# Row sums added to a row of the column products by two transfers, in place of a spread on a diagonal

## The chip, the cores and the metric

The kernel runs on one core of a Trainium2 chip. Its engines work side by side, each through its own list of instructions in order: TensorE (PE, matmuls), VectorE (DVE), ScalarE (ACT), GpSimd (POOL) and SyncE (SP, which here only issues transfers). The metric is the device time of one execution in microseconds (us); less is better.

## The reference

Input `x` is 4 images of 64 channels of 256x256 numbers. Layer 0 convolves each channel with its own long 2-D filter `k`, an outer product of two decaying curves that small networks make from `z` (`hx`, `hy`), and adds a bias:

```python
k = einsum('ijk,imk->ijmk', hx, hy)            # one separable filter per channel
out = irfft2(rfft2(x) * rfft2(k) / fft_size) + x * bias[:, None, None]
```

Layer 1 weighs the products of the rows of each image with each other, sums them, adds the sum to each row, and normalises the channel:

```python
scores = einsum('bpsd,bptd->bpst', x, x) / sqrt(256)
red = sum(scores * weights[None], axis=-1, keepdims=True)
y = x + red
y_hat = (y - mean) * rsqrt(var + 1e-5)         # mean, var over images, rows, columns
return y_hat * gamma + beta
```

## The kernel before

The 64 channels are handled one after another in a loop (lines 662 to 709); the last two run through `last_channels` with an order of their own. Within a channel the filter's separability makes the convolution two rounds of matmuls with triangular Toeplitz blocks (`toep`): `conv_z` (line 211) into `z`, copied out of PSUM by ACT (line 220), and `conv_x0` (line 236), to which DVE adds the bias (line 246), giving `x0`.

`gram` (line 299) multiplies the rows of `x0` with each other, in two halves `v`, two images in each, into PSUM. The scores are symmetric, so only some blocks of 64x64 are computed. `weigh` then uses each block twice: once summed along its rows (line 328, two instructions per image, whose accumulated sums go to two columns of `red0`), and once as products that are still to be summed down the columns (line 319, into `pr`, 256 numbers per partition and image).

The two kinds of sum are put together as follows. `spread` (line 340, four instructions of 128x128 after each half) multiplies the identity by the two row sums, so that each partition's row sum lies on the diagonal, and adds `pr`, into `sp`. `all_sum` (line 348) is one all-reduce over the partitions on GpSimd, of 1024 numbers each: it gives all partitions the full sums, `rd`. In the next iteration of the loop ACT copies half of `rd` in place (`pick_red`, line 357), and DVE adds `rd` to `x0` with two passes of 128x1024 (`add_red`, line 364), which also accumulate the channel's sum. A small all-reduce (line 368) follows, then on ACT the mean (lines 411 and 412) and the squares (line 416), on GpSimd `sum_squares` (line 422), and later the root, the newton steps and the output (`finish`, line 462).

The order on every engine is written out by hand (`tc.manual_schedule()`): an engine takes its instructions as the program lists them and waits at the first that isn't ready. For DVE and channel c that is: adding the bias (four instructions), newton steps of channel c-3, weighing and spreading of c's first half, `add_red` of c-1, weighing and spreading of c's second half. For POOL: `sum_squares` of c-2, the small reduction of c-1, `all_sum` of c. For ACT, `pick_red` of c-1 stands behind the copies of `z` and ahead of the root of c-2.

All matmul results share a pool `ps` of eight PSUM banks, given out in turn, two each for the two halves of `conv_x0`, of `conv_z` and of `gram`. `sp`, `pr` and `rd` have two buffers each. SP issues all loads and stores of the loop. The channels from 61 on (`BY_PE`) use matmuls for the sums instead, except that the first half of 61 still goes through `spread` and `all_sum`.

Of the kernel before, what the change touches and what calls it, by code (L numbers as in the profile page):

```python
# [8 lines left out]
F32 = mybir.dt.float32  # L9
AF = mybir.ActivationFunctionType  # L10
ALU = mybir.AluOpType
# [4 lines left out]
B, C, S = 4, 64, 256  # L16
P = 128
# [20 lines left out]
def conv_scores_bn_kernel(  # L38
# [19 lines left out]
    nc = tc.nc  # L58

    const = ctx.enter_context(tc.tile_pool(name="const", bufs=1))  # L60
    dram = ctx.enter_context(tc.tile_pool(name="dram", bufs=1, space=DRAM))
    ld = ctx.enter_context(tc.tile_pool(name="ld", bufs=3))
    wk = ctx.enter_context(tc.tile_pool(name="wk", bufs=2))
    sm = ctx.enter_context(tc.tile_pool(name="sm", bufs=3))
# [3 lines left out]
    def load_xt(c, v, n):  # L68
        if not n:
            xts[c, v] = ld.tile([P, 4, S], F32, tag=f"xt{v}", name=f"xt_{c}_{v}", bufs=4)  # L70
        part = bass.ts(n, 2)
        nc.sync.dma_start(xts[c, v][:, part], xT[c, v, :, part])
# [45 lines left out]


    g_dram = dram.tile([COPIES, C, 2, GW], F32, name="g_dram")  # L120

    hs[0] = ld.tile([P, 2, GW], F32, tag="toep", name="toep_0")
    with tc.tile_pool(name="fps", bufs=4, space=PSUM) as fps:
# [54 lines left out]
    def load_h(c, n):  # L178


        if not n:
            hs[c] = ld.tile([P, 2, GW], F32, tag="toep", name=f"toep_{c}")
        src = bass.AP(
            g_dram.tensor, g_dram.offset + c * 2 * GW + 16 * n,
            [[4 + C * 2 * GW, COPIES], [1, 4], [1, GW + S]],
        )
        rows = hs[c][bass.ts(n, 16)].rearrange("p a r -> p (a r)")
        nc.sync.dma_start(rows[:, : GW + S], src)

    def copy_h(c):  # L190

        toep = hs[c]
        nc.scalar.copy(toep[H:, :, :S], toep[:H, :, :S])  # L193
# [5 lines left out]
    st8, zs = {}, {}  # L199
# [22 lines left out]
    def conv_x0(c, z, parts=range(2)):  # L222


        toep = hs[c]
        if not c:
            first_x0(z)
            return
        for m in parts:
            p2 = [ps.tile([P, 2, S], F32, tag="ps", name=f"p2_{c}_{m}_{v}") for v in range(2)]  # L230
            for i in range(2):
                for k in range(4):
                    for t in range(4):
                        v, u = t % 2, t // 2
                        rows = bass.ts(v, H)
                        nc.tensor.matmul(  # L236
                            p2[v][bass.ts(u, H), i, : S - H * k],
                            lhsT=z[rows, u, k, bass.ts(2 * m + i, H)],
                            rhs=toep[rows, 0, H * k : S], start=(k == 0), stop=(k == 3),
                        )  # L240
            add_bias(c, m, p2)
# [31 lines left out]

    def begin(c):
        x0 = wk.tile([P, 2, 4, S], F32, tag="x0", name=f"x0_{c}", bufs=5)
        red0 = sm.tile([P, B, 2], F32, tag="red0", name=f"red0_{c}")
        sp = wk.tile([P, B, S], F32, tag="sp", name=f"sp_{c}")
        pr = wk.tile([P, B, S], F32, tag="pr", name=f"pr_{c}")
        rd = wk.tile([P, B, S], F32, tag="rd", name=f"rd_{c}")
        st8[c] = (x0, red0, sp, pr, rd)  # L280
# [3 lines left out]
    def gram(c, v, weighed=True):  # L284


        xb = st8[c][0].rearrange("p v i (t s) -> p v i t s", s=H)
        gs = [ps.tile([P, 8, H], F32, tag="ps", name=f"g_{c}_{v}_{u}") for u in range(2)]

        for places in (  # L290
            ((0, slice(0, 3), slice(0, 5, 2)), (1, slice(1, 4), slice(2, 7, 2))),
            ((2, slice(2, 4), slice(3, 7, 3)), (3, slice(0, 4, 3), slice(0, 4, 3))),
        ):
            for i in range(4):
                for n in range(4):
                    u, h = n % 2, n // 2
                    rows = bass.ts(u, H)
                    m, t, o = places[h]
                    nc.tensor.matmul(  # L299
                        gs[u][bass.ts(h, H), o, :],  # L300
                        lhsT=xb[rows, v, i, m, :], rhs=xb[rows, v, i, t, :],
                        start=(i == 0), stop=(i == 3),
                    )
        if not weighed:
            banks.extend(gs)
            return
        for u in range(2):
            weigh(c, 2 * v + u, gs[u])
        if c < BY_PE or (c == BY_PE and not v):
            for u in range(2):  # L310
                spread(c, 2 * v + u)

    def weigh(c, b, g, rows_last=True):

        _, red0, _, pr, _ = st8[c]
        w = ws[c]

        def products():
            nc.vector.scalar_tensor_tensor(  # L319
                pr[:, b].rearrange("p (t s) -> p t s", s=H), g[:, COL, :], 1.0 / math.sqrt(S),  # L320
                w[:, 6:10, :], ALU.mult, ALU.mult,
            )

        if not rows_last:
            products()
        for n, part in enumerate((ROW0, ROW1)):
            junk = wk.tile([P, 3, H], F32, tag="junk", name=f"junk_{c}_{b}_{n}")
            nc.vector.scalar_tensor_tensor(  # L328
                junk, g[:, part, :], 1.0 / math.sqrt(S), w[:, 3 * n : 3 * n + 3, :],
                ALU.mult, ALU.mult, accum_out=red0[:, b, n : n + 1],  # L330
            )
        if rows_last:
            products()

    def spread(c, b):

        _, red0, sp, pr, _ = st8[c]
        for n in range(2):
            part = bass.ts(n, P)
            nc.vector.scalar_tensor_tensor(  # L340
                sp[:, b, part], eye_sb, red0[:, b, n : n + 1], pr[:, b, part],
                ALU.mult, ALU.add,
            )

    def all_sum(c, part=slice(0, B)):

        _, _, sp, _, rd = st8[c]
        nc.gpsimd.partition_all_reduce(  # L348
            rd[:, part].rearrange("p b s -> p (b s)"), sp[:, part].rearrange("p b s -> p (b s)"),
            P, RED.add,  # L350
        )
# [20 lines left out]
    BY_PE = C - 3  # L372
# [37 lines left out]
    def minus_mean(mom):  # L410
        nc.scalar.activation(mom[:, 4:5], mom[:, 2:3], AF.Identity, bias=mom[:, 3:4])  # L411
        nc.scalar.activation(mom[:, 5:6], mom[:, 4:5], AF.Identity, scale=-1.0 / (B * S * S))

    def squares(c, mom, v):
        sq = wk.tile([P, 4, S], F32, tag="sq", name=f"sq_{c}_{v}", bufs=1)
        nc.scalar.activation(  # L416
            sq, st8[c][0][:, v], AF.Square, bias=mom[:, 5:6], accum_out=mom[:, 6 + v : 7 + v]
        )
# [24 lines left out]
    def scale_shift(c, mom, v, r):  # L443
        return scale_shift_of(c, mom, newton(c, v, r))
# [204 lines left out]
    def parts_of(c, place):  # L649

        e, f = c - 4, c - 3
        parts = [[(e, 0, 1)], [(e, 1, 0)], [(e, 1, 1)], [(f, 0, 0)], []]
        if c >= C - 4:
            parts[4] = [(f, 0, 1)]
        if c == C - 3:
            parts[0] = []
            parts[4] += [(f, 1, 0), (f, 1, 1)]
        for i, v, n in parts[place]:
            if i >= 0:
                finish(*fins[i], v, n)  # L660

    for c in range(C - 2):
        p, q, f = c - 1, c - 2, c - 3
        begin(c)
        copy_h(c + 1)
        parts_of(c, 0)
        if c + 2 < C and c:
            load_xt(c + 2, 1, 1)
        load_h(c + 2, 0)
        conv_x0(c, zs.pop(c))  # L670
        if q >= 0:
            minus_mean(moms[q])
            squares(q, moms[q], 0)
        parts_of(c, 1)
        if c + 3 < C:
            load_xt(c + 3, 0, 0)
        load_h(c + 2, 1)
        if q >= 0:
            squares(q, moms[q], 1)
            tot = sum_squares(q, moms[q])  # L680
        if f >= 0:
            fins[f] = (f, *scale_shift(f, moms.pop(f), *scales.pop(f)))
        begin_z(c + 1)
        copy_z(c + 1, 0, conv_z(c + 1, 0))
        parts_of(c, 2)
        load_h(c + 2, 2)
        if c + 3 < C:
            load_xt(c + 3, 1, 0)
        load_w(c + 1)
        load_h(c + 2, 3)  # L690
        copy_z(c + 1, 1, conv_z(c + 1, 1))
        if p >= 0:
            pick_red(p)
        parts_of(c, 3)
        if c + 3 < C:
            load_xt(c + 3, 0, 1)
        if q >= 0:
            scales[q] = root(q, tot)
        if c == C - 3:
            copy_h(c + 2)  # L700
        parts_of(c, 4)
        gram(c, 0)
        if p >= 0:
            moms[p] = add_red(p)
        if c == BY_PE:
            all_sum(c, slice(0, 2))
        gram(c, 1)
        if c < BY_PE:
            all_sum(c)
    last_channels(C - 1)  # L710

# [70 lines left out]
```

## Time and profile before

Three runs took 883.51, 889.34 and 885.22 us (median 885.22). The profiled execution:

| | us | share of the span |
|---|---|---|
| span, first to last instruction | 872.5 | |
| PE busy | 855.9 | 98% |
| DVE busy | 755.9 | 87% |
| ACT busy | 621.9 | 71% |
| POOL busy | 427.8 | 49% |
| `all_sum`, 62 times | 376.8, 6.08 each | |
| `spread`, 492 instructions | 139.0, 0.34 each | |

The page gives the profiled execution's span; the median of the runs lies 12.7 us above it, for what stands around the first and last instruction. A busy time counts an instruction from its start to its end, and neighbours on one engine overlap a little: four spreadings of 0.34 take 1.13 together. In the timeline a line has start, duration, engine, line, operation and `out<-in`; in square brackets stand the idle time of the engine before it and what ended it. An engine name with a q (SPq, ACTq) is the queue's issuing of a transfer, not its landing.

### The profile page before, as it was taken

What the parts mean: (1) busy time and instruction counts of PE and PEld (TensorE: products, weight loads), DVE (VectorE), ACT (ScalarE), POOL (GpSimd) and SP (SyncE); (2) the same over time, 40 slices, a digit from 0 to 9 for tenths busy, and PEclk for the clock granted to TensorE, in tenths of its full rate; (3) what the DMA queues carried; (4) which work ended last, traced back from release to release, by engine and by line L of the source; (5) the groups of instructions that cost most, each with busy time, mean ns of one, the idle gap of its engine ahead of it and who ended that gap; (6) DMA issues with size and microseconds to landing.
All of it is one profiled execution on the core that took longest, in us unless ns stands there. A gap on an engine that the chain in (4) does not pass through costs nothing.

```text
span 872.5 us, 55963 instructions
## 1 busy us (share of the span) xinstructions
PE 855.9 (98%) x24674; PEld 836.2 (96%) x24674; DVE 755.9 (87%) x2647; ACT 621.9 (71%) x1218; POOL 427.8 (49%) x194
## 2 busy tenths in 40 slices
PE   7999999999999999999999999999999999999995
PEld 5999999999999999999999999999999999999994
DVE  3588988988988988988998998998998988988996
ACT  2256767767767767777777777777777767767786
POOL 0236546546546546546546546546546546546530
PEclk9999999999999999999999999999999999999997
DMA  6724665565565556565565565655555655565535
GB/s 189 221 77 139 198 209 195 201 211 193 201 210 192 200 196 206 202 207 193 203 208 192 203 206 194 205 200 199 203 201 199 202 203 192 204 210 193 190 141 194
DMA packets 89870, 169.69 MB, mean 194 GB/s; under 512 B 10555, under 2 KB 11740, under 8 KB 89628
## 3 DMA queue, kind: packets, MB, share of 16 engines
q1 hardware_dynamic: 88972, 165.52, 55.6%
q8 instruction: 194, 3.18, 1.6%
q10 hardware_dynamic: 656, 0.59, 0.3%
q14 instruction: 48, 0.39, 0.2%
HBM read 98.18 MB, written 67.76 MB: 190 GB/s over the span
## 4 chain that ended last, share of the span: by engine, by line
PE 97%; DVE 2%; DMA 1%; issue 0%; ACT 0%; DVEq 0%; ACTq 0%
PE p L211 32%; PE g L299 32%; PE p L236 32%; PE p L265 0%; DMA toep<-g_sb 0%; PE ph L132 0%; DVE junk L328 0%; DMA zw_sb<-in_zw 0%; PE rp L379 0%; DVE fa L135 0%; DVE x L516 0%; DVE pr L319 0%; PE rp L384 0%; PE s L507 0%; DVE fa L140 0%
## 5 line engine op out<-in xcount | busy, mean ns | idle before, releaser
L348 POOL PARTITION_ALL_REDUCE rd<-sp x62 | 376.8, 6078 | 182.4 <-DVE sp L340 182.4
L211 PE MATMUL p<-toep,xt 64*64 64x256 f32 (+3 forms) x8192 | 304.0, 296 | 0.9 <-DMA toep<-g_sb 0.9
L299 PE MATMUL g<-x 64*64 64x192 f32 (+1 forms) x8192 | 302.5, 296 | 0.0
L211 PEld LDWEIGHTS p<-toep,xt 64*64 64x64 f32 x8192 | 291.4, 133 | 8.6 <-PE idle L168 1.5
L236 PE MATMUL p<-toep,z 64*64 64x256 f32 (+3 forms) x8064 | 298.3, 296 | 0.0
L236 PEld LDWEIGHTS p<-toep,z 64*64 64x64 f32 x8064 | 289.6, 133 | 6.8 <-issue 0.2
L299 PEld LDWEIGHTS g<-x 64*64 64x64 f32 x8192 | 289.7, 133 | 0.8 <-DVE x L246 0.2
L328 DVE SCALAR_TENSOR_TENSOR junk<-g,w 128x192 f32<-128x192 f32 x512 | 160.9, 351 | 81.1 <-PE g L299 77.7
L462 ACT ACTIVATE o<-x,sh,g 128x512 f32<-128x512 f32 x252 | 203.3, 810 | 3.0
L246 DVE SCALAR_TENSOR_TENSOR x<-xt,chan_sb,p 128x512 f32<-128x512 f32 x256 | 173.8, 739 | 7.6 <-PE p L265 7.2
L220 ACT COPY z<-p 128x512 f32<-128x512 f32 x256 | 134.7, 576 | 22.3 <-PE p L211 22.3
L416 ACT ACTIVATE sq<-x,mom 128x1024 f32<-128x1024 f32 x127 | 145.2, 1143 | 3.3 <-DVE x L405 1.1
L364 DVE SCALAR_TENSOR_TENSOR x<-x,rd 128x1024 f32<-128x1024 f32 x122 | 144.1, 1218 | 0.0
L340 DVE SCALAR_TENSOR_TENSOR sp<-eye_sb,red,pr 128x128 f32<-128x128 f32 x492 | 139.0, 344 | 0.0
L368 POOL PARTITION_ALL_REDUCE mom<-mom x61 | 24.5, 401 | 231.1 <-DVE x L364 227.1
L357 ACT COPY rd<-rd 64x512 f32<-64x512 f32 (+1 forms) x62 | 38.0, 612 | 134.8 <-POOL rd L348 134.7
L319 DVE SCALAR_TENSOR_TENSOR pr<-g,w 128x256 f32<-128x256 f32 x256 | 107.3, 419 | 0.0
L193 ACT COPY toep<-toep 64x512 f32<-64x512 f32 x63 | 38.9, 617 | 32.0 <-DMA toep<-g_dram 26.7
L411 ACT ACTIVATE mom<-mom 128x1 f32<-128x1 f32 x62 | 18.2, 293 | 38.0 <-POOL mom L368 37.1
L328 DVE DVE_READ_ACCUMULATOR junk<-g,w 128x1 f32 x512 | 42.2, 82 | 0.0
L422 POOL PARTITION_ALL_REDUCE tot<-mom x62 | 29.8, 481 | 5.1 <-ACT sq L416 5.1
L416 ACT ACTIVATION_READ_ACCUMULATOR sq<-x,mom 128x1 f32 x127 | 23.7, 186 | 0.0
(84 smaller groups left out, 220.4 us busy)
## 6 DMA issues: line engine op xcount, KB each, us to landing
xt<-in_xT SPq DMA_DIRECT2D x256, 256.0 KB
out<-o SPq DMA_DIRECT2D x256, 256.0 KB
w<-in_wl SPq DMA_DIRECT2D x64, 320.0 KB
toep<-g_dram SPq DMA_DIRECT2D x252, 36.0 KB
g_dram<-g_sb SPq DMA_DIRECT2D x1, 320.0 KB
g_dram<-g_sb ACTq DMA_DIRECT2D x1, 320.0 KB
decay_sb<-in_decay SPq DMA_DIRECT2D x1, 256.0 KB
fw_sb<-in_fw ACTq DMA_DIRECT2D x1, 192.0 KB
```

What stands on the lines that cost most here:

```text
L211: nc.tensor.matmul(p1[u][bass.ts(v, H), k, : S - H * i], lhsT=xts[c, v][rows, i, bass.ts(2 * m + k, H)], rhs=toep[rows, 1, H * i : S], sta ...
L220: nc.scalar.copy(zs[c][:, u, bass.ts(m, 2), :], p1[u][:, :, ::-1])
L236: nc.tensor.matmul(p2[v][bass.ts(u, H), i, : S - H * k], lhsT=z[rows, u, k, bass.ts(2 * m + i, H)], rhs=toep[rows, 0, H * k : S], start=(k ...
L246: nc.vector.scalar_tensor_tensor(st8[c][0][:, v, part], xts[c, v][:, part], chan_sb[:, 0, c : c + 1], p2[v][:, :, ::-1], ALU.mult, ALU.add,)
L299: nc.tensor.matmul(gs[u][bass.ts(h, H), o, :], lhsT=xb[rows, v, i, m, :], rhs=xb[rows, v, i, t, :], start=(i == 0), stop=(i == 3),)
L319: nc.vector.scalar_tensor_tensor(pr[:, b].rearrange("p (t s) -> p t s", s=H), g[:, COL, :], 1.0 / math.sqrt(S), w[:, 6:10, :], ALU.mult, A ...
L328: nc.vector.scalar_tensor_tensor(junk, g[:, part, :], 1.0 / math.sqrt(S), w[:, 3 * n : 3 * n + 3, :], ALU.mult, ALU.mult, accum_out=red0[: ...
L340: nc.vector.scalar_tensor_tensor(sp[:, b, part], eye_sb, red0[:, b, n : n + 1], pr[:, b, part], ALU.mult, ALU.add,)
L348: nc.gpsimd.partition_all_reduce(rd[:, part].rearrange("p b s -> p (b s)"), sp[:, part].rearrange("p b s -> p (b s)"), P, RED.add,)
L364: nc.vector.scalar_tensor_tensor(x0[:, v], x0[:, v], 1.0, rd[:, 2 * v, None, :].to_broadcast([P, 4, S]), ALU.mult, ALU.add, accum_out=mom[ ...
L416: nc.scalar.activation(sq, st8[c][0][:, v], AF.Square, bias=mom[:, 5:6], accum_out=mom[:, 6 + v : 7 + v])
L462: nc.scalar.activation(o, y, AF.Identity, bias=sh, scale=g)
```

## The change

The spreading is left out for the channels below 61. Instead, the row sums of a channel are gathered in a 128x32 tile, of which eight columns are used (four images by two); there are three such tiles in turn, set to zero once at the start. One DVE instruction turns this tile in blocks of 32x32. GpSimd's queue stores the turned tile (128 rows of 32 numbers, 16 KB) to DRAM, and a second transfer from the same queue reads from there the eight rows of each of the four blocks, in the order in which `pr` has its 1024 numbers, and adds them to partition 0 of `pr` (`accum_op`). `all_sum` then sums `pr` itself. Since one partition's row now carries all row sums, the sum over the partitions is the same as before. `add_rows` stands behind the second half's weighing and ahead of `all_sum`; the first transfer waits for DVE, the second for the first, and `all_sum` for the second.

```diff
     g_dram = dram.tile([COPIES, C, 2, GW], F32, name="g_dram")
+    reds = [const.tile([P, 32], F32, name=f"reds_{n}") for n in range(3)]
+    for tile_ in reds:
+        nc.vector.memset(tile_, 0.0)
...
-        red0 = sm.tile([P, B, 2], F32, tag="red0", name=f"red0_{c}")
+        red0 = reds[c % 3][:, : 2 * B].rearrange("p (b n) -> p b n", n=2)
...
-        if c < BY_PE or (c == BY_PE and not v):
+        if c == BY_PE and not v:
             for u in range(2):
                 spread(c, 2 * v + u)
...
+    def add_rows(c):
+        across = sm.tile([P, 32], F32, tag="across", name=f"across_{c}", bufs=2)
+        nc.vector.transpose(across, reds[c % 3])
+        rows = dram.tile([P, 32], F32, name=f"rows_{c}")
+        nc.gpsimd.dma_start(rows, across)
+        pr = st8[c][3]
+        nc.gpsimd.dma_start(
+            pr[0:1].rearrange("p b (n q i) -> p (b n) q i", n=2, i=32),
+            rows.rearrange("(q j) i -> j q i", q=4)[None, : 2 * B], accum_op=ALU.add,
+        )
+
     def all_sum(c, part=slice(0, B)):
-        _, _, sp, _, rd = st8[c]
+        _, _, sp, pr, rd = st8[c]
+        if c < BY_PE:
+            sp = pr
...
         gram(c, 1)
         if c < BY_PE:
+            add_rows(c)
             all_sum(c)
     last_channels(C - 1)
```

## The prediction

> **What bounds the kernel now.** I read the page's busy times and its chain first, because they say which engine a saving would have to reach:
>
> ```profile
> PE 855.9 (98%) x24674; PEld 836.2 (96%) x24674; DVE 755.9 (87%) x2647; ACT 621.9 (71%) x1218; POOL 427.8 (49%) x194
> ...
> PE 97%; DVE 2%; DMA 1%; issue 0%; ACT 0%; DVEq 0%; ACTq 0%
> ```
>
> TensorE is nearly full and is 97% of the chain that ended last. VectorE, from which the change takes work, is 2% of it. Then I cut one channel out of the middle with a table by stretches. The longest matmul pieces of the chain start every 13.08 us (404.32, 417.40, 430.48), so I asked for a stretch of that length:
>
> ```profile
> 413.08:426.16 13.08, 13.08 (x390) 12.89 (x384) 11.71 (x42) 9.73 (x20) 6.92 (x3) 1.00 0.58 197
> ```
>
> The columns are length, then busy time of PE, PEld, DVE, ACT and POOL, granted clock and DMA share. PE is busy for all 13.08 us: the period is PE's. DVE has 1.37 us free and POOL half of its time. A kernel bound like this gains nothing from a lighter DVE, and it loses once some other loop takes longer than 13.08 us per channel. So the question is whether there is such a loop, and how much room it has. I followed one channel's row-and-column sums through the timeline of that stretch, engine by engine (start, duration):
>
> ```profile
> 417.81 1.13 DVE L340 SCALAR_TENSOR_TENSOR sp<-eye_sb,red,pr 128x128 f32<-128x128 f32 x4
> ...
> 425.77 1.13 DVE L340 SCALAR_TENSOR_TENSOR sp<-eye_sb,red,pr 128x128 f32<-128x128 f32 x4
> 426.82 1.22 DVE L364 SCALAR_TENSOR_TENSOR x<-x,rd 128x1024 f32<-128x1024 f32 x1
> ...
> 429.11 0.35 DVE L328 SCALAR_TENSOR_TENSOR junk<-g,w 128x192 f32<-128x192 f32 x1
> ```
>
> ```profile
> 419.11 6.12 POOL L348 PARTITION_ALL_REDUCE rd<-sp  x1 [2.43 <-DVE sp L340]
> ```
>
> ```profile
> 425.26 0.62 ACT L357 COPY rd<-rd 64x512 f32<-64x512 f32 x1 [2.29 <-POOL rd L348]
> ```
>
> They form a **ring** that closes every channel, since DVE runs its instructions in the written order: second weighing of channel c ends (417.81), spreading, all-reduce, copy on ACT (`pick_red`), the two passes of `add_red`, second weighing of c+1, which ends at 430.89. Its lengths: 1.13 spreading, 0.17 to POOL's start, 6.15 until ACT starts, 0.62 copy, 0.94 in which the result lies ready while DVE is still spreading (425.88 to 426.82), 2.29 for `add_red` (426.82 to 429.11), 1.78 for the weighing. The sum is 13.08, so the ring has only **0.94 us** to spare.
>
> **The change part by part.**
>
> *Removed:* eight spreadings per channel for c below 61, four after each half. Four take 1.13 us, so DVE gets 2.26 us per channel back, 138 us in 61 channels. The four of the first half lie beside the all-reduce and gave only the 0.94 us of waiting; the second four lie in the ring, which gets 1.13 us shorter. By themselves both are worth nothing, because PE's 13.08 us stay.
>
> *Added on DVE:* one 32x32 transpose of 128x32 numbers. No row shows one; a memset of 128x64 takes 0.11 and the products of 128x256 take 0.42. I take 0.2, nearer the row of like size. The three memsets at the start lie where DVE waits for loads: nothing.
>
> *Added on POOL's queue, in the ring:* a store of the turned 16 KB to DRAM, and a second transfer that reads 4 KB of them back and adds them into one row of `pr`. The second waits for the landing of the first, and the all-reduce for the landing of the second. The two latencies D therefore stand one after the other in front of the 6.12 us, with nothing beside them on POOL; behind the waiting transfers stand the all-reduce, then `sum_squares` of two channels earlier (0.48) and the small reduction of `add_red` (0.40). ACT waits at `pick_red` and DVE at `add_red`.
>
> The trace has no transfer issued by POOL and none that accumulates. The nearest rows for a transfer as small as these, from issue to the start of the waiting instruction, are these. With the chip nearly quiet, 2 KB of `fb_sb` are issued at 0.73, and DVE starts on them at 2.72, 1.99 us:
>
> ```profile
> 0.73 0.40 ACTq L87 DMA_DIRECT2D fb_sb<-in_fb  x1
> ```
>
> ```profile
> 2.72 0.15 DVE L124 TENSOR_SCALAR turns<-fb_sb 128x1 f32<-128x1 f32 x1 [1.42 <-DMA fb_sb<-in_fb]
> ```
>
> In the full stream (DMA share 0.58), the last piece of a `toep`, issued behind 576 KB of other loads on the same queue, goes out at 424.38 and is used at 428.00, 3.62 us:
>
> ```profile
> 424.38 0.63 SPq L188 DMA_DIRECT2D toep<-g_dram  x1
> ```
>
> ```profile
> 428.00 0.62 ACT L193 COPY toep<-toep 64x512 f32<-64x512 f32 x1 [0.58 <-DMA toep<-g_dram]
> ```
>
> So D lies between 2 x 1.99 = 3.98 and 2 x 3.62 = 7.24; a gain is excluded, since the second can't begin before the first has landed. POOL's queue has no large loads ahead of it, which pulls to the lower end; the other queue's traffic on the same engines, runs of only 128 bytes, and an accumulation that also reads its target pull up. I take the middle, 2.8 each, **D = 5.6**.
>
> *The new ring:* 0.2 transpose + 0.17 to POOL + D + 6.15 + 0.62 + 0.1 to DVE (an estimate beside the 0.17 from DVE to POOL) + 2.29 + 1.78 = 11.31 + D = **16.91 us**. That is 3.83 us over PE's 13.08.
>
> *Can the ring be opened elsewhere?* The eight banks of PSUM go round in the order X0, X1, Z0, Z1, G0, G1 (two banks each), so the next Z1 needs the banks of the weighed G1. After a weighing PE has Z1 and G0 to do (2.18 each), and DVE then weighs G0 (1.78): 6.2 us, while `add_red` starts 16.91 - 2.29 - 1.78 = 12.84 us after it. PE, the adding of the bias and the newton steps are all done by then, and ACT's work of 9.73 us fits too. So every microsecond of D above 1.77 (13.08 - 11.31) is lost.
>
> *The sum:* channels 0 to 60 are added by rows, which makes 60 periods: 60 x 3.83 = 230 us. In the first channel the result had 3.3 us to spare (copy done at 44.20, `add_red` at 47.50), and all-reduce moves by 4.75 (0.2 + 0.17 + 5.6 after 36.20, instead of 37.42): +1.4. At the end PE stands about one half-stage (2.2) further ahead of DVE than before: -2.2. Together +229 us. On the profiled execution's span this is 872.5 + 229 = 1101.5. The median is 885.2, 12.7 above that span, and I add the same 12.7 for what lies around it: 1114 us.
>
> Two rules of the Trainium skill bear on this; no number above or below needs them. "DMA: Bandwidth & Descriptors", section on the anatomy of a GpSimd-issued DMA, puts a small one at about 2.0 us fixed, most of it the receipt of the write; the quiet row's 1.99 agrees, the loaded row's 3.62 does not, and no row shows one from GpSimd. An estimate by that page would be D = 4.0, a ring of 15.3 us and about 1018 us. "TensorE: Matmul & The Clock Gate", Part 1, says that an idle window of about 3.4 us halves the array's clock until a busy window restores it. The trace's granted clock is 1.00 in each full stretch and 0.91 over the last 52 us, where PE is busy for 42. Since PE would now stand still about 3.8 us per channel, that rule could bite in some channels; by it, Z1, G0 and the weighing after would take 10.5 us instead of 6.2, still inside 12.84, so the sum stays.
>
> **The rivals.**
>
> *The transfers are dearer* (chance 0.13). POOL writes each transfer's descriptors itself and may pay for the change between all-reduce and transfers; accumulation may be slow. For it: POOL's instructions are the least known of this trace. Against: the 6.12 us of the all-reduce stay the same whatever runs before. With D above 7.7 the time is above 885 + 60 x (19.0 - 13.08) = 1240; D = 10 gives about 1378.
>
> *They are cheaper than a quiet transfer* (0.05): D between 2 and 4 gives 900 to 1018. Against it is that two landings are waited for, each of which takes 1.99 us on a quiet chip.
>
> *Not slower* (0.03): one mechanism, the two transfers in POOL's queue ahead of all-reduce. If they passed on in 1.77 us together (under 0.9 each), the ring would be 13.08 and PE would hide it: 885 us. For it: only 16 and 4 KB. Against: half of the quickest transfer in the trace.
>
> *DVE sets the pace after all* (0.01): then 61 x 2.26 = 138 us would be won, 747 us. PE's full stretches say no.
>
> **How the numbers follow.** The forecast, D from 3.98 to 7.7 (the loaded pair and half a microsecond for the accumulation, which no row shows), has a chance of 0.78, and its ends are 1018 and 1240; I put the low end at 1015. What is left out is 0.13 above and 0.09 below. The time of the likeliest case is 1114. Slower by over 1% takes in the forecast and the dearer and cheaper cases, 0.96; within 1%, which is about what a measurement of this kernel can tell from no change, 0.03; faster 0.01.
>
> **What the changed profile would show.** PE busy some 77% of each period, and a period near 17 us; the chain no longer PE's but POOL, DMA, ACT and DVE in turn; DVE's first `add_red` pass waiting for ACT's copy; all-reduce waiting for a transfer and no longer for DVE, at an unchanged 6.1 us; POOL issuing 122 transfers; 492 spreadings of L340 gone but for four. Wrong would be: a period of 13.08 with the transfers hidden; an all-reduce that itself gets longer; a lower granted clock with PE at the end of the chain.

## The result and the profile after

The changed kernel takes **1200.97 us** (median; 1198.86 to 1209.10) against 884.37 us (882.25 to 889.34): 1.3596 times as long, interval 1.3531 to 1.3662. The forecast was 1114 us, the range 1015 to 1240.

From the page of the changed kernel, the busy times, then the shares of the chain that ended last:

```profile
PE 968.6 (81%) x24674; PEld 919.0 (77%) x24674; DVE 639.4 (53%) x2223; ACT 628.3 (52%) x1218; POOL 517.1 (43%) x316
...
DMA 33%; POOL 31%; DVE 14%; issue 13%; PE 5%; ACT 3%; DVEq 0%; POOLq 0%; ACTq 0%
```

PE was 97% of the chain and is 5%. Two thirds of the chain are now transfers and POOL. (PE's busy time has grown without a matmul more; that comes further down.) The groups of the ring, with the idle time ahead of each and what ended it:

```profile
L365 POOL PARTITION_ALL_REDUCE rd<-pr x61 | 372.8, 6112 | 162.5 <-DMA pr<-rows 162.5
L381 DVE SCALAR_TENSOR_TENSOR x<-x,rd 128x1024 f32<-128x1024 f32 x122 | 144.6, 1222 | 368.2 <-ACT rd L374 368.2
L374 ACT COPY rd<-rd 64x512 f32<-64x512 f32 (+1 forms) x62 | 37.9, 611 | 492.2 <-POOL rd L365 492.2
...
L355 POOL DMA_DIRECT2D pr<-rows x61 | 53.5, 878 | 180.4 <-DMA rows<-across 176.0
...
L353 POOL DMA_DIRECT2D rows<-across x61 | 36.4, 597 | 134.0 <-DVE across L351 134.0
```

The all-reduce is as long as before (6.11 us), but it waits for a transfer and no longer for DVE. The second transfer waits for the first; ACT's copy waits 492 us for the all-reduce; the passes of `add_red`, which never stood still before, wait 368 us for that copy. One channel in the timeline, first POOL's three steps (start, duration, in brackets the idle time before and its end), then the ring's other steps:

```profile
604.38 0.59 POOL L353 DMA_DIRECT2D rows<-across  x1 [1.63 <-DVE across L351]
...
607.23 0.88 POOL L355 DMA_DIRECT2D pr<-rows  x1 [2.25 <-DMA rows<-across]
...
609.79 6.11 POOL L365 PARTITION_ALL_REDUCE rd<-pr  x1 [1.68 <-DMA pr<-rows]
...
615.93 0.61 ACT L374 COPY rd<-rd 64x512 f32<-64x512 f32 x1 [6.89 <-POOL rd L365]
...
616.58 1.22 DVE L381 SCALAR_TENSOR_TENSOR x<-x,rd 128x1024 f32<-128x1024 f32 x1 [5.91 <-ACT rd L374]
...
620.66 0.20 DVE L351 STREAM_TRANSPOSE across<-reds 128x32 f32<-128x32 f32 x1
```

This is one of the quick channels: 2.85 us from the first issue to the second, 2.56 from there to the all-reduce, and 16.78 from one transpose (603.88) to the next. In the same way I read all 61 channels off POOL's timeline. The first landing (issue to issue) takes 3.55 us in the mean (2.81 to 5.09), the second (issue to all-reduce) 3.54 (2.15 to 5.91), and from the end of the all-reduce to the next first issue it is 5.25 in every channel. The period is 18.45 us: 3.55 + 3.54 + 6.11 + 5.25. Sixty of them are 60 x (18.45 - 13.08) = 322 us over the old period; the spans differ by 1197.1 - 872.5 = 324.6, the medians by 316.6. A landing here is always read in the profiled execution; between runs that do the same with it, its mean scatters by some 0.2 us (the first one 3.34 to 3.70).

### The profile page after: what moved, and what is told of

Read it like the earlier page. It is cut to its first block, busy times and chain, and to the rows that moved or that the text cites. A ratio compares the mean times of both kernels' runs of the same rounds, so it can differ in the third digit from the quotient of the medians.

```text
span 1197.1 us, 55785 instructions
## 1 busy us (share of the span) xinstructions
PE 968.6 (81%) x24674; PEld 919.0 (77%) x24674; DVE 639.4 (53%) x2223; ACT 628.3 (52%) x1218; POOL 517.1 (43%) x316
## 4 chain that ended last, share of the span: by engine, by line
DMA 33%; POOL 31%; DVE 14%; issue 13%; PE 5%; ACT 3%; DVEq 0%; POOLq 0%; ACTq 0%
POOL rd L365 31%; DMA pr<-rows 17%; DMA rows<-across 15%; DVE x L381 6%; DVE junk L331 5%; ACT rd L374 3%; PE p L214 2%; PE g L302 1%; DVE across L351 1%; DVE pr L322 1%; PE p L239 1%; PE p L268 0%; DMA fw_sb<-in_fw 0%; PE idle L171 0%; PE rp L396 0%
## 5 line engine op out<-in xcount | busy, mean ns | idle before, releaser
L214 PE MATMUL p<-toep,xt 64*64 64x256 f32 (+3 forms) x8192 | 418.8, 354 | 211.8 <-ACT toep L196 211.2
L214 PEld LDWEIGHTS p<-toep,xt 64*64 64x64 f32 x8192 | 369.4, 163 | 247.5 <-ACT toep L196 229.4
L365 POOL PARTITION_ALL_REDUCE rd<-pr x61 | 372.8, 6112 | 162.5 <-DMA pr<-rows 162.5
L302 PE MATMUL g<-x 64*64 64x192 f32 (+1 forms) x8192 | 305.6, 296 | 0.0
L239 PE MATMUL p<-toep,z 64*64 64x192 f32 (+3 forms) x8064 | 301.6, 296 | 0.0
L239 PEld LDWEIGHTS p<-toep,z 64*64 64x64 f32 x8064 | 290.7, 133 | 7.6 <-issue 0.2
L355 POOL DMA_DIRECT2D pr<-rows x61 | 53.5, 878 | 180.4 <-DMA rows<-across 176.0
L353 POOL DMA_DIRECT2D rows<-across x61 | 36.4, 597 | 134.0 <-DVE across L351 134.0
```

The costliest lines, as they stand in the source:

```text
L214: nc.tensor.matmul(p1[u][bass.ts(v, H), k, : S - H * i], lhsT=xts[c, v][rows, i, bass.ts(2 * m + k, H)], rhs=toep[rows, 1, H * i : S], sta ...
L239: nc.tensor.matmul(p2[v][bass.ts(u, H), i, : S - H * k], lhsT=z[rows, u, k, bass.ts(2 * m + i, H)], rhs=toep[rows, 0, H * k : S], start=(k ...
L302: nc.tensor.matmul(gs[u][bass.ts(h, H), o, :], lhsT=xb[rows, v, i, m, :], rhs=xb[rows, v, i, t, :], start=(i == 0), stop=(i == 3),)
L365: nc.gpsimd.partition_all_reduce(rd[:, part].rearrange("p b s -> p (b s)"), sp[:, part].rearrange("p b s -> p (b s)"), P, RED.add,)
```

## The experiments

All times stand beside runs of the kernel before on the same chip (medians 881.8 to 883.6 us). "Landings" are read as above, means over 61 channels.

### Without the row sums

```diff
         if c < BY_PE:
-            add_rows(c)
             all_sum(c)
```

> The changed kernel without the transpose and without both transfers; the all-reduce sums the column products alone, so the row sums are missing from the output. Ring theory (the loss is the two landings in front of the all-reduce, and the lighter DVE is worth nothing): the ring is 18.45 - 0.2 - 7.1 - 0.1 = about 11.0 us, PE's 13.08 set the period again, 885 us within 3. Rival, DVE's load counts: 2.26 us less of DVE work per channel show, anything clearly below 880 us. Rival, something else of the change costs time (the zeroed tiles, the all-reduce reading the products): above 890 us.

Measured: 884.77 us, ratio 1.0016 (0.9983 to 1.005). Its page, busy times and chain:

```profile
PE 859.1 (98%) x24674; PEld 832.5 (95%) x24674; DVE 628.2 (72%) x2162; ACT 627.8 (72%) x1218; POOL 427.8 (49%) x194
...
PE 97%; DVE 1%; DMA 1%; issue 0%; ACT 0%; DVEq 0%; ACTq 0%
```

DVE is 128 us lighter than in the kernel before (755.9), and nothing comes of it. All of the loss lies in the transpose and the two transfers.

### One landing instead of two

```diff
+    rows_0 = dram.tile([P, 32], F32, name="rows_0")
+    nc.gpsimd.dma_start(rows_0, reds[0])
...
-        rows = dram.tile([P, 32], F32, name=f"rows_{c}")
-        nc.gpsimd.dma_start(rows, across)
...
-            rows.rearrange("(q j) i -> j q i", q=4)[None, : 2 * B], accum_op=ALU.add,
+            rows_0.rearrange("(q j) i -> j q i", q=4)[None, : 2 * B], accum_op=ALU.add,
```

> The first transfer of every channel is left out (the second reads a tile of zeros that was stored once at the start, so the row sums are missing); transpose, second transfer and all waits behind it stay. Ring theory: the ring loses the 3.55 us from the first issue to the second, 18.45 - 3.55 = 14.9 us, 885 + 60 x 1.82 = 994 us (980 to 1010). If the loss came from POOL's issuing or from ACT and PE waiting for each other, and the landings lay beside that: much less than 200 us are won, above 1100 us.

Measured: 977.74 us, ratio 1.1059 (1.1002 to 1.1117), a little under the range. From its page, the all-reduce and the transfer that is left, which now waits for DVE and for no other transfer:

```profile
L365 POOL PARTITION_ALL_REDUCE rd<-pr x61 | 372.6, 6108 | 145.7 <-DMA pr<-rows 145.7
...
L355 POOL DMA_DIRECT2D pr<-rows x61 | 53.4, 875 | 141.2 <-DVE across L353 141.2
```

The one landing left takes 3.26 us, the period is 14.76. Taking one landing out wins 223 us: the landings stand in series with everything else in the ring.

### A shorter all-reduce

```diff
-            all_sum(c)
+            all_sum(c, slice(0, 2))
...
-                x0[:, v], x0[:, v], 1.0, rd[:, 2 * v, None, :].to_broadcast([P, 4, S]),
+                x0[:, v], x0[:, v], 1.0, rd[:, 0, None, :].to_broadcast([P, 4, S]),
```

(`pick_red` copies the one pair of sums into both places.)

> The changed kernel with an all-reduce of half the width: only the first two images' sums are made and added to all four, so the sums of the others are missing. Passes, copies and transfers keep their sizes. Ring theory: 6.11 becomes the 3.32 us that the half-width all-reduce of channel 61 takes, every term of the ring counts in full, the ring is 18.45 - 2.79 = 15.66 us, the time 1201 - 60 x 2.79 = 1034 us (1020 to 1045). Rival, the loop closes elsewhere (ACT with PE behind it, or POOL's own load): less than half of that, above 1110 us.

Measured: 1027.95 us, ratio 1.1604 (1.1523 to 1.1685), as the ring expects. From POOL's timeline of this run:

```profile
613.62 0.88 POOL L355 DMA_DIRECT2D pr<-rows  x1 [2.95 <-DMA rows<-across]
617.81 3.23 POOL L365 PARTITION_ALL_REDUCE rd<-pr  x1 [3.32 <-DMA pr<-rows]
```

The all-reduce takes 3.23 us, 2.88 less, and the period falls from 18.45 to 15.61, 2.84 less. A term that the change doesn't touch counts in full too, so it is the ring that sets the pace.

### ACT's copy for PE ahead of the copy that waits

```diff
         begin(c)
-        copy_h(c + 1)
+        if not c:
+            copy_h(c + 1)
         parts_of(c, 0)
...
+        copy_h(c + 2)
         if p >= 0:
             pick_red(p)
         parts_of(c, 3)
...
-        if c == C - 3:
-            copy_h(c + 2)
```

> The changed kernel, but ACT copies the next channel's Toeplitz half (line 196) ahead of the copy that waits for the all-reduce, instead of two instructions behind it. PE no longer waits for it (211 us of PE's idle time in the changed kernel end with it) and should stand still less in one piece. Ring theory: PE had room to wait, so the time stays 1201 us within 10, while PE's idle time moves to other releasers and the granted clock rises from 0.90. Rival, the loss is PE held up behind ACT, with the lower clock after each stop: the time falls by 60 us or more, towards 1000 to 1140 us.

Why this was tried: in the changed kernel PE's idle time ends with ACT's Toeplitz copy, which stands behind `pick_red` in ACT's order. In the view of waits (total us, times, longest), first of the changed kernel, then of this run:

```profile
PE p L214 <- ACT toep L196: 211.2, 59, 7.4
```

```profile
PE p L214 <- DVE pr L322: 166.6, 56, 5.3
```

Measured: 1185.17 us, ratio 1.3368 (1.3302 to 1.3434). The releaser that PE had is gone, and PE now waits for the weighing that frees its banks. The granted clock rises as expected, from 0.90 to 0.91. The time falls by only 16 us, more than the ring's own "within 10" and far from the rival's 60. The landings of this run sum to 6.90 us instead of 7.09, which is within their scatter; the period is 18.24 instead of 18.45, and 60 x 0.21 = 13 us are that difference. PE held up behind ACT was not the loss.

### Writing instead of adding

```diff
-            rows.rearrange("(q j) i -> j q i", q=4)[None, : 2 * B], accum_op=ALU.add,
+            rows.rearrange("(q j) i -> j q i", q=4)[None, : 2 * B],
```

> The second transfer writes its 4 KB over partition 0 of the products instead of adding to it, so that row of the products is lost; all waits stay. If accumulation is what makes the second transfer as long as the first (3.54 us from issue to all-reduce in the mean, for a quarter of the bytes), that stretch falls to about 2.8 us or less and the time by 60 x 0.7 = 42 us or more, to 1159 us or below. If a landing costs the same whatever it does: 1201 us within 10, and 3.5 us again.

Measured: 1169.36 us, ratio 1.3223 (1.3136 to 1.3311): between the two. The second landing falls from 3.54 to 3.03, the first stays at 3.54. POOL's instruction for the second transfer, which took 878 ns where it accumulates, in this run:

```profile
L355 POOL DMA_DIRECT2D pr<-rows x61 | 34.7, 568 | 180.6 <-DMA rows<-across 180.6
```

Accumulation costs 0.51 us per channel, of which 0.31 are POOL's own instruction, and 31.6 us of the whole. It is a part of the price and not the main one.

### One hop without DRAM

```diff
-        rows = dram.tile([P, 32], F32, name=f"rows_{c}")
-        nc.gpsimd.dma_start(rows, across)
         pr = st8[c][3]
-        nc.gpsimd.dma_start(...)
+        row = pr[0:1].rearrange("p b (n q i) -> p (b n) q i", n=2, i=32)
+        for q in range(4):
+            nc.gpsimd.dma_start(
+                row[:, :, q], across[32 * q : 32 * q + 2 * B, None, :], accum_op=ALU.add,
+            )
```

> The same sums with one hop: four accumulating transfers of 1 KB each, one per block of 32 partitions, straight from the turned tile into partition 0 of the products, without DRAM and without a wait between them. Theory: landings in series cost, landings side by side don't; POOL issues three more (0.88 each), then one accumulating landing as before (3.54): 3 x 0.88 + 3.54 = 6.2 instead of 7.09 us, 1201 - 60 x 0.9 = 1147 us (1110 to 1165). If the bytes or the small pieces set the price, four transfers cost more than two: above 1201 us.

Measured: 1138.98 us, ratio 1.2895 (1.2836 to 1.2954), as expected. POOL's timeline of this run, with the four issues merged in one line:

```profile
403.86 3.28 POOL L355 DMA_DIRECT2D pr<-across  x4 [1.88 <-DVE across L351]
409.85 6.11 POOL L364 PARTITION_ALL_REDUCE rd<-pr  x1 [2.71 <-DMA pr<-across]
```

In this channel four issues (3.28) and one landing after them (2.71) are 5.99 us. In the mean it is 6.63 us from the transpose to the all-reduce, instead of 7.59 in the changed kernel. Four transfers without a wait between them are cheaper here than two with one; that they also don't go through DRAM isn't parted from it. This is the cheapest way found to keep the whole change in the ring, and it still costs 255 us.

### The first transfer from SP

```diff
-        nc.gpsimd.dma_start(rows, across)
+        nc.sync.dma_start(rows, across)
```

> The changed kernel with the first transfer issued by SP instead of POOL; the second, which accumulates, stays with POOL. If POOL's writing of a transfer's descriptors is a good part of a landing (0.59 us of busy time and 0.28 before it), the first landing falls by up to 0.8 us and the time by up to 48 us, to 1150 us. If SP's queue, where the transfer stands behind the loads and SP's own waits, costs as much (the loaded row of the kernel before, 3.62 us): 1201 us within 15; if SP is itself kept waiting at a store, above 1215 us.

Measured: 1181.65 us, ratio 1.3408 (1.3316 to 1.35): 1.6% better, the end of "within 15" passed by 4 us. The period of the profiled execution, the slowest of the four (1191.93), is 18.34 us, 0.11 less; the medians differ by 0.3 us per channel. The single landings can't be parted in this run: POOL's second issue begins 2.55 us after SP's in the mean, instead of 3.55, but the all-reduce follows it by 4.70, instead of 3.54. So SP in POOL's place wins at most 0.3 of the 0.87 us that were put down to POOL's issuing. What POOL's issuing alone costs isn't shown, since SP's has a price too.

### What the traffic does to a landing

Three runs of the changed kernel with less traffic:

```diff
# few stores (and in the run with both)
-        queue.dma_start(out[c, v, n], o)
+        if not v and not n:
+            queue.dma_start(out[c, v, n], o)
# few loads (and in the run with both), in load_xt
+        if c >= 4:
+            xts[c, v] = xts[c - 4, v]
+            return
```

> The changed kernel with only one in four of the output stores issued (the first quarter of each channel; the others are computed and not stored): 48 of 171 MB less through the DMA engines. If the other queue's traffic stretches the two landings, their sum of 7.09 us per channel falls: taking the excess over two quiet landings, 7.09 - 3.98 = 3.1, as proportional to the bytes, to about 6.2, and the time by 60 x 0.9 to about 1148 us. If a landing of a transfer issued by POOL costs 3.5 us with or without traffic: 1201 us within 12.

> The changed kernel, but the image loads (xt) of channels 4 to 63 are left out; they compute with the images of channels 0 to 3 again: 63 MB of 171 less. Leaving out 48 MB of stores left the sum of both landings at 7.17 us, so bytes alone don't set it. If it is the loads, issued in a burst just as the landings are waited for, that stretch them, the sum falls from 7.09 to about 5.0 to 6.2 us, the time to 1075 to 1150 us. If a landing has this price whatever runs beside it: 1201 us within 15.

> Both left out: the image loads from channel 4 on and three in four output stores, 111 of 171 MB less. If traffic is what makes 7.1 us out of two landings, the sum comes near its shortest cases in the changed kernel (2.81 + 2.15 = 4.96 us), the ring near 16.3 us and the time near 1073 us (1030 to 1100). If not, 1201 us within 20.

| run | MB moved | us | ratio (interval) | first landing | second | sum | period |
|---|---|---|---|---|---|---|---|
| changed | 171 | 1200.97 | 1.3596 (1.3531, 1.3662) | 3.55 | 3.54 | 7.09 | 18.45 |
| few stores | 121 | 1192.69 | 1.3485 (1.3419, 1.3551) | 4.27 | 2.90 | 7.17 | 18.52 |
| few loads | 108 | 1127.54 | 1.2787 (1.2740, 1.2835) | 2.86 | 3.06 | 5.92 | 17.27 |
| both | 58 | 1152.45 | 1.3060 (1.3009, 1.3112) | 3.68 | 2.73 | 6.41 | 17.77 |

The run with few loads lies where the effect of the loads was expected. The run with few stores lies within 12 us of the changed kernel and doesn't differ from it by more than the runs scatter. The run with both lies in neither of its ranges. The periods are 11.35 us above the sums in every row, so the period follows the landings and nothing else. The landings don't follow the bytes: with fewest bytes the time is longer than with fewer loads alone. The lists of DMA issues give the reason's place (KB each, median us from issue to landing), few loads first, then both:

```profile
rows<-across POOLq DMA_DIRECT2D x61, 16.0 KB, 1.9
pr<-rows POOLq DMA_DIRECT2D x61, 4.0 KB, 3.0
```

```profile
rows<-across POOLq DMA_DIRECT2D x61, 16.0 KB, 2.8
pr<-rows POOLq DMA_DIRECT2D x61, 4.0 KB, 2.3
```

The first landing is dear where the second is cheap. I sorted the landings by whether SP issued a channel's weights (`w`, 320 KB) between 2 us before the landing's start and 1 us before its end. In the changed kernel the second landing takes 3.96 us in the 32 channels with it and 3.08 in the 29 without; with few loads, 3.67 (23) and 2.69 (38). This way of sorting favours long landings, since a later end takes in more issues. Sorted by the start alone (weights issued from 2 us before it to 1.5 us after it), the difference stays: 4.29 us in 15 channels and 3.30 in the other 46, with few loads 3.73 (15) and 2.84 (46). In the two runs with few stores SP issues one store per channel instead of four, the loads behind it go out closer together, and the weights go out in the first landing in all 61 channels: those are the 4.27 and 3.68, and the second landings, free of it, are the 2.90 and 2.73. One channel of the run with few stores, POOL's two transfers and SP's issue of the weights between them:

```profile
611.40 0.59 POOL L353 DMA_DIRECT2D rows<-across  x1 [1.63 <-DVE across L351]
...
614.67 0.88 POOL L355 DMA_DIRECT2D pr<-rows  x1 [2.68 <-DMA rows<-across]
```

```profile
612.12 0.38 SPq L78 DMA_DIRECT2D w<-in_wl  x1
```

This sorting is an observation and not an experiment of its own: no run leaves out the weights alone. Some spread stays unexplained: in the run with both, the DMA engines are on average 6% busy during the second landing, and it takes 2.15 to 4.14 us. What makes that difference is open.

### The ring opened

```diff
-            add_rows(c)
-            all_sum(c)
+            store_rows(c)              # transpose and first transfer
+            if late(c):                # c < 58
+                if c:
+                    all_sum(c - 1)
+                fetch_rows(c)          # second transfer
+            else:
+                fetch_rows(c)
+                all_sum(c)
...
-        p, q, f = c - 1, c - 2, c - 3
+        if c == LAST:                  # 58
+            catch_up(c)
+        p, q, f = c - 1 - late(c), c - 2 - late(c), c - 3 - late(c)
```

(`x0` has six buffers instead of five, `pr` three instead of two. `catch_up` does the mean, squares, root and outputs of the channels that are one behind, and `add_red` of one, without new matmuls.)

> The changed kernel with the same transfers, opened at the ring: up to channel 57 POOL makes the all-reduce of a channel one channel later, between the two transfers of the next one, and everything from the copy of the sums on comes one channel later too (one more buffer for x0 and for the products); before channel 58 one piece of work without matmuls catches up. Ring theory: no result is waited for, PE's 13.08 us set the period, 885 us and some 7 for the catching up, 885 to 900 us. Rival, the transfers themselves or their issuing disturb the other work (traffic, POOL's time, the buffers): above 910 us.

Measured: 906.78 us, ratio 1.0275 (1.0228 to 1.0322), above the expected 900. The period was 13.08 us in most channels up to 57 (13.2 in the mean); I had left the three channels after it out of the sum, which still had the ring. So the next run takes them out:

```diff
-        if c == BY_PE and not v:
+        if LAST <= c < BY_PE or (c == BY_PE and not v):
             for u in range(2):
                 spread(c, 2 * v + u)
...
```

> The run with the late all-reduce, but channels 58 to 60, which there still had both landings in the ring, put their row sums on the diagonal as the kernel before does. In that run the period was 13.08 us up to channel 57 and the 22 us over the kernel before came after it. Ring theory: three rings of 18.3 us go (3 x 5.2 = 16 us), the catching up stays (some 7 us), 906.8 - 16 = 891 us (886 to 897). Rival, the transfers slow the rest a little in every channel: 900 us or more.

Measured: 896.52 us, ratio 1.0164 (1.0119 to 1.0209), at the expected range's upper end. A table by stretches of this run (length, busy PE, PEld, DVE, ACT, POOL, clock, DMA share, GB/s):

```profile
400.00:413.08 13.08, 13.08 (x385) 12.97 (x381) 9.37 (x34) 9.85 (x20) 8.26 (x6) 1.00 0.62 198
...
790.00:804.00 14.00, 4.32 (x124) 3.86 (x116) 7.33 (x25) 7.58 (x15) 9.29 (x6) 0.80 0.33 116
```

With the same transfers in every channel up to 57 PE is full again in the middle: from 40 to 790 us it is busy for 746.9 of 750. But a busy PE is not yet a PE at its old pace. From the first matmul of L214 for channel 2 to that for channel 57 this run takes 729.3 us, the run without the row sums 723.3 and the kernel before (L211 there) 719.8. Most of these channels take 13.08 us in all three; the rest take up to 14.3 here. So outside the ring the transfers cost 55 channels at most 9.5 us, 0.17 each, and not all of that need be theirs: the run without transfers is 3.5 us behind, too. The one stop at the catching up shows in PE's timeline:

```profile
804.28 2.25 PE L214 MATMUL p<-toep,xt 64*64 64x256 f32 x22 [9.96 <-ACT toep L196]
```

With the slower matmuls after it (117 of them take 6.45 us, where 122 took 4.42 before the stop) this channel takes 25.50 us instead of 13.08. These 12.4 us are most of the 14.8 between the medians. The rival, that the transfers slow every channel a little, is bounded by this and not excluded. What costs 317 us in the ring costs less than 10 out of it.

No version here beats the kernel before: PE's 13.08 us remain, and no run with the ring closed comes near them.

## Why the prediction was right

- **What bounds:** that PE's 13.08 us stay and the lighter DVE is worth nothing held (run without the row sums, 1.0016). The rival in which DVE sets the pace is out.
- **The ring and its terms** held. Against the working's 11.31 + D the runs show 11.35 + D: the transpose 0.20 as taken; from DVE to POOL's issue 0.30 (604.08 to 604.38) instead of 0.17, and from ACT to DVE about 0.03 instead of 0.1. That it is additive was shown from both sides, with a landing taken out and with a shorter all-reduce.
- **D is the term that was mis-sized:** 7.09 us instead of 5.6, close to the loaded pair's 7.24. 60 x 1.49 = 89 us are the whole distance between 1114 and 1201. Two things I named had been given too little: accumulation (0.51, shown by the run that writes) and the other traffic (1.17 of the two landings go with the image loads left out). My argument for the middle, that nothing large stands ahead in POOL's own queue, was wrong in its weight: the large loads of SP's queue slow the landings all the same. How the rest of the landings divides isn't shown. Even with the DMA engines 6% busy, the second landing takes 2.73 us, not the 1.99 of the quiet row, so the lower bound was too low for this kind of transfer. By the page's estimate of 2.0 us each, which the prediction took from "DMA: Bandwidth & Descriptors", the sum would have been 1018 us; no run here has a mean landing as short as that.
- **Whether the ring can be opened elsewhere:** here a wait was overlooked. I had PE waiting only for the banks of the weighed half; it waited first for ACT's Toeplitz copy behind `pick_red`. That it changed no number was luck, since I hadn't worked out its room. The run with the early copy shows that it had room: with that wait gone, the one I had named appears in its place, and the time stays but for the landings.
- **The clock:** the granted clock fell from 0.994 to 0.899, and the matmuls that come right after the stop are the ones that got longer. By form, mean ns in third place, first the kernel before, then the changed kernel:

```profile
L211 PE MATMUL p<-toep,xt 64*64 64x256 f32 x2048 | 207.2, 377 | 0.9 <-DMA toep<-g_sb 0.9
```

```profile
L214 PE MATMUL p<-toep,xt 64*64 64x256 f32 x2048 | 312.4, 470 | 211.8 <-ACT toep L196 211.2 <-DVE pr L322 0.3 <-DVE across L351 0.3
...
L239 PE MATMUL p<-toep,z 64*64 64x256 f32 x2016 | 215.6, 377 | 0.0
```

  The stage after the stop takes 470 ns instead of 377, the same form two stages later (L239) 377 as ever. This goes with the rule cited from "TensorE: Matmul & The Clock Gate", Part 1 (half rate after an idle window, full rate after a busy one). It makes PE's busy time 113 us longer and the kernel no slower: from the end of the all-reduce to the next first issue it is 5.25 us in every channel, at whatever clock, so all of it lies in PE's room, as the sum had it.
- **The bridge** of 12.7 us from span to median was misread: it isn't what stands around the first and last instruction. The changed kernel's profiled execution took 1199.04 us for a span of 1197.1, and the timed runs of the kernel before lie 1.8 us above their own spans (883.59 for 881.8). So the profiled execution of before took about 874 us and was quicker than the three timed ones. The forecast doesn't change by it, since 885.2 + 229 is 1114 all the same.
- **The rivals:** "dearer" began at D of 7.7 and wasn't reached; "cheaper" and "not slower" are out.

## What to carry to other kernels

Before moving work off an engine, find the loop that each channel closes and its room; here it was 0.94 us, though GpSimd was idle half of the time, and a full TensorE hid it. A transfer that is small in bytes is not small in a ring: each landing that was waited for cost 2.7 to 4.3 us in the means of these runs, two in series the sum, and it seems to count which large load goes out beside it. If such a hop is needed, take it out of the ring by one channel's delay, where the same transfers cost under 0.2 us per channel here, or issue several without a wait between them.

## What the runs showed that I had not expected

- Fewer bytes can make a landing longer: with 29% fewer bytes the first landing went from 3.55 to 4.27 us. In that run SP issues the weights earlier, into the landing; that this is the cause is argued, not shown.
- A PE that the profile shows as busy throughout can still fall behind: 746.9 of 750 us busy in the last run, and up to 9.5 us later after 55 channels.
- An accumulating transfer costs POOL 0.88 us to issue, a plain one of the same form 0.57.
- Landings vary from channel to channel by a factor of two and more (2.15 to 5.91 us), and not only with traffic; why is open.
